# Gathers of a graph kernel's node table, counted on 68 semaphores of their own in turn, with TensorE's wait set by hand

## The chip, the cores and the metric

One Trainium2 chip, of which the kernel uses one core. The metric is the device time of one execution in microseconds (us), as the median of several runs. About 0.2% is what a measurement of this kernel can tell from no change.

The engines are named as in the profile: PE (TensorE) multiplies matrices, PEld is its loading of the stationary operand, DVE (VectorE) and ACT (ScalarE) work elementwise, POOL (GpSimd) here issues gathers, and SP (SyncE) issues plain transfers. Each engine runs its own instructions in order and is tied to the others by semaphores: counters which one side raises and the other waits for.

## The reference

A pre-norm layer of a relational graph network. There are 12500 nodes of 256 features, 212500 edges sorted by their target, and 8 types of edges, each with a 256x256 weight.

```python
hx = jnp.einsum('ni,rio->rno', x, weight)
msg = hx[edge_type, src]
agg = jax.ops.segment_sum(msg, dst, num_segments=num_nodes)
node_repr = agg * jnp.asarray(ALPHA, x.dtype) ** 0.5
node_repr = node_repr + h_bias
loop_message = x @ loop_weight
node_repr = node_repr + loop_message * jnp.asarray(1.0 - ALPHA, x.dtype) ** 0.5
...
h = jnp.maximum(_layernorm(x, axis=-1), 0.0)
x = x + _L0_gnn_ref(edge_index, h, edge_type_8, weight, h_bias, loop_weight)
```

## The kernel before

The kernel turns the order round: it first sums the rows of h over each target's incoming edges, apart for each type, and then multiplies these sums by the weights.

**Tiles.** The edges are cut into 1581 tiles of up to 128 edges; two tiles (PAIR) make a unit that belongs to one stretch of neighbouring targets. For a tile three things are needed. Its 128 source rows of 256 numbers (128 KB) come by a *gather*: one indirect DMA that POOL issues (`gather`, L901, with the DMA at L915), from x for the first 100 tiles, while the table h is still being made, and from h later. A one-hot matrix (`onehots`, L957), made by DVE for four tiles at once, says for each edge which target and type it counts for. Then PE (`edge_sums`, L985) multiplies the two: for each half c of the features one matmul at L1005, so two in the code for a tile. The profile shows four matmuls and four weight loads, since each of these in float32 runs as two. A unit's two tiles sum in one PSUM bank; after the unit DVE adds the bank into the accumulator ring `acc` (`add_sums`, L1021, the addition at L1031).

**Groups.** When a group of 128 targets has all its sums, PE multiplies them by the eight weights and by the self-loop weight (`group_work`, L1172, matmuls at L1187), and DVE adds the result to x and it is stored.

**The order of work** is written out by hand, in one loop over tiles (L1363). At tile t it issues the gathers up to `goal(t)` (L922): 64 tiles ahead until tile 170, then fewer, down to 24 from tile 370 on, and in the last 120 tiles a fifth of what is left, not under 8. A gather of an even tile also waits for the last finished unit (L918-920, "no faster than the sums"). The message buffers hold 66 tiles in pairs.

**Row tiles.** Every 28th tile from tile 167 on (167, 195, ..., 50 in all) is not gathered by POOL. Its 128 rows are fetched by 128 transfers of 1 KB each, half from SP and half from ACT (`load_sources`, `fetch`). They count on four semaphores `rows0` to `rows3`, for which PE waits in an instruction of its own at L1002. So POOL issues 1581 - 50 = 1531 gathers, 1431 of them from h.

**Semaphores of the gathers.** The kernel names none for them. The scheduler under it counts the DMAs of POOL on eight semaphores in turn, and sets a gather's waits itself: for the DMA that counted on the same semaphore before, eight gathers earlier, and for PE where a buffer or the pace asks for it. An instruction holds one wait; a second one becomes an instruction of its own in front of it. The first matmul of a gathered tile waits on the gather's semaphore for its full count (16 for each DMA).

**Runs.** `in_run` (L358) ties the matmuls of a unit together: only the last counts on PE's semaphore, and whoever waits for the unit waits for that count.

Of the kernel before, what the change touches and what calls it, by code (L numbers as in the profile page):

```python
# [66 lines left out]
HOLD = 8  # L67
FAR = 36
COUNTERS = 4


QUAD = 4
# [172 lines left out]
def kernel(  # L245
# [15 lines left out]
    KC = D // P  # L261
# [48 lines left out]
    def place_of(t):  # L310
        u, i = divmod(t, PAIR)
        half = 0 if PAIR * u + 1 == NT else PAIR - 1 - i
        b, row = row_of(u)
        return b, half, row


    with ExitStack() as main:
# [29 lines left out]
        msg, oh, offsets, kind = {}, {}, {}, {}  # L347
        firsts, stops, loops, marked, typed, gidx, col = {}, {}, {}, {}, {}, {}, {}
        added, zeroed = {}, {}
        single, fetches = {}, {SP: [], ACT: []}  # L350
        counters = [tc.alloc_semaphore(f"rows{i}") for i in range(COUNTERS)]
        fetched, summed = {}, {}
        state = {"h32": None}


# [2 lines left out]
        def in_run(kind, i, last):  # L358

            name, count = runs.get(kind, (None, 0))  # L360
            key = f"{kind}{count}"
            if last:
                if name is not None:
                    tc.declare_fence(i.ins, group=key)
                runs[kind] = (None, count + 1)
            else:
                tc.no_tile_sem_insts.add(i.ins.name)
                tc.add_to_no_dep_group(key, i.ins)
                runs[kind] = (key, count)
            return i  # L370
# [508 lines left out]
        def room(t):  # L879

            both = msgs.tile([P, PAIR, D], F32, name="msg")
            for i in range(PAIR):
                msg[t + i] = both[:, i, :]

        def single_rows(t):

            return (t % SINGLE == SINGLE - 1 and t + 2 * NEAR < NT
                    and state["h32"] is not None and t // QUAD * QUAD >= state["h32"] + LATE + AHEAD)

        def begin_fetch(t):  # L890

            if t not in msg:
                room(t - t % PAIR)
            fetched[t] = len(fetched)
            for k, r in enumerate(range(0, P, SOURCES)):
                engine = SP if k in BY_SP else ACT
                fetches[engine].append((
                    done["tile"] + HOLD,
                    lambda r=r, engine=engine: load_sources(t, r, engine)))

        def gather(t):  # L901
            if t % PAIR == 0 and t not in msg:
                room(t)
            if t % QUAD:
                kind[t] = kind[t - 1]
            else:
                kind[t] = "h" if state["h32"] is not None and t >= state["h32"] + LATE else "x"
            table = {"h": h32, "x": x}[kind[t]]
            b, i, u = place_of(t)
            if single_rows(t) and t not in fetched and t - done["tile"] >= FAR:  # L910
                begin_fetch(t)
            if t in fetched:
                return
            at = i * P + u
            i = nc.gpsimd.indirect_dma_start(  # L915
                out=msg[t], out_offset=None, in_=table[:, :],
                in_offset=bass.IndirectOffsetOnAxis(ap=gidx[b][:, at : at + 1], axis=0))
            if "unit" in latest:  # L918
                tc.add_manual_dep(
                    i.ins, latest["unit"], SYNC_DEP, reason="no faster than the sums")  # L920
# [7 lines left out]
        def load_sources(t, r0, engine):  # L928
# [9 lines left out]
            def fetch_row(i, v):  # L938
                j = queue.dma_start(
                    msg[t][r0 + i : r0 + i + 1, :].bitcast(U8), h32_bytes[:, bass.ds(v, D * 4)])  # L940
                j.then_inc(counters[k % COUNTERS], 16)
                tc.no_tile_sem_insts.add(j.ins.name)
                tc.add_to_no_dep_group(f"rows{t}", j.ins)
                if i == 0 and k >= COUNTERS:
                    tc.add_manual_dep(
                        j.ins, summed[k - COUNTERS], SYNC_DEP, reason="counter is at rest")

# [37 lines left out]
        def edge_sums(t):  # L985
            m, o = msg.pop(t), oh.pop(t)
            if t % PAIR == 0:
                bank = banks[t // PAIR % BANKS]
                sums["ps"] = bank[:, : KC * R * WIN].rearrange("p (c k) -> p c k", c=KC)
            ps = sums["ps"]  # L990
            i = t % PAIR
            b, half, _ = place_of(t)
            first, width = (R * n for n in (REACH[half] if b < NB - 1 else (0, WIN)))
            end = t == NT - 1 or i == PAIR - 1
            free = added.get(t // PAIR - BANKS)
            if i == 0 and free is not None and latest["pe"] is not None:
                tc.add_manual_dep(latest["pe"], free.name, SYNC_DEP, reason="bank is free")
            if i == 0 and latest["pe"] is not None:
                tc.add_manual_dep(latest["pe"], made[t], SYNC_DEP, reason="one-hots are made")
            if t in fetched:  # L1000
                k = fetched[t]
                j = nc.tensor.wait_ge(counters[k % COUNTERS], 16 * P * (k // COUNTERS + 1))  # L1002
                tc.declare_fence(j.ins, group=f"rows{t}")
            for c in range(KC):
                j = nc.tensor.matmul(  # L1005
                    ps[:, c, first : first + width], m[:, c * P : (c + 1) * P], o[:, :width],
                    start=(i == 0 and c == 0), stop=(end and c == KC - 1), skip_group_check=True)
                in_run("sums", j, end and c == KC - 1)
            latest["pe"] = j.ins
            if end:  # L1010
                latest["unit"] = j.ins.name
            if t in fetched:
                summed[fetched[t]] = j.ins.name
            return ps

        sums = {}
# [216 lines left out]
        with tc.manual_schedule():  # L1233
# [20 lines left out]
            for t in range(min(STARTED, NT)):  # L1254
                gather(t)
            gathered = min(STARTED, NT)

            for bound, lines in ((low, plan.low), (high, plan.high)):
                whole = small.tile([P, NB], I32, name="whole")
                f = small.tile([P, NB], F32, name="bound_f")  # L1260
# [102 lines left out]
            for t in range(NT):  # L1363
# [3 lines left out]
                while gathered < min(NT, goal(t)):  # L1367
                    gather(gathered)
                    gathered += 1
# [31 lines left out]
                if t % (PAIR * REGS) == 0 and t // PAIR + REGS < NU:  # L1401
                    load_offsets(t // PAIR + REGS)
                ps = edge_sums(t)
                while late and late[0][0] <= t:
                    late.pop(0)[1]()
                    credit -= 0.83
                advance(t)
                while writes and credit > 0:
                    _, cost, f = writes.pop(0)
# [14 lines left out]
                while queue and (budget > 0 and t >= queue[0][0] or t >= queue[0][1]):  # L1424
                    _, _, c, f = queue.pop(0)
# [67 lines left out]
```

## Time and profile before

| | |
|---|---|
| median of 3 runs | 1981.88 us (1979.95 to 1982.96) |
| profiled execution | 1982.09 us, its span 1980.4 us, mean granted clock of TensorE 0.949 |
| DMA of the gathers (queue 0) | 200.77 MB, 34.5% of 16 engines' span |
| DMA issued by SP and ACT (queues 1 and 10) | 76.03 MB, 12.8% |

The page gives for each engine its busy time and share of the span. Its groups of instructions have the form: line, engine, operation, out<-in, how many; then busy time in us, mean ns of one; then the idle time of the engine just before them and the releaser that ended most of it. "issue" as a releaser means that the profile shows nothing that the engine waited for. On POOL the length of a gather is the time in which its descriptors are made, not that of the transfer. Views over a stretch of time give the same for that stretch alone.

### The profile page before, as it was taken

The page shows a single profiled execution, that of the slowest core. Times are in us where ns is not written, and L with a number is a line of the kernel's source. Part 1 is how long each engine was busy: PE and PEld are TensorE (multiplying, and loading weights), DVE is VectorE, ACT ScalarE, POOL GpSimd, SP SyncE. Part 2 cuts the span into 40 slices and gives each one's busy share as a digit, 9 for nine tenths or more (in the row PEclk, how much of TensorE's full clock was granted, in tenths as well). Part 3 has the DMA queues.
Part 4 walks back from the last instruction along what each step waited for, and adds up shares of the span by engine and source line. Part 5 has one row for each costly group of instructions (what it writes and reads, how often), then busy time and mean ns, then how long its engine had stood idle before and what let it go on. Part 6 is the DMA issues. An engine that isn't in the chain of part 4 may idle for free. (4 is left out here: it accounts for less than half of the span.)

```text
span 1980.4 us, 41340 instructions
## 1 busy us (share of the span) xinstructions
PE 1711.7 (86%) x10161; PEld 1473.8 (74%) x10161; DVE 1309.2 (66%) x3272; ACT 159.2 (8%) x334; POOL 1457.9 (74%) x1557
## 2 busy tenths in 40 slices
PE   2348999998899888889998898888989989899998
PEld 1247898997777777778777777777777767687897
DVE  6769767886665677656678565578666567665653
ACT  6777200000000000000000000000000000000000
POOL 7677776677777777777777777777777777777774
PEclk8559999999999999999999999999999999999999
DMA  7993444443444444444434444444444344444432
GB/s 252 358 301 103 126 126 134 140 140 107 138 128 122 149 132 120 141 130 121 149 111 141 132 119 143 141 119 141 129 122 142 109 144 130 120 140 125 127 115 78
DMA packets 158363, 279.45 MB, mean 141 GB/s; under 512 B 35376, under 2 KB 109126, under 8 KB 158118
## 3 DMA queue, kind: packets, MB, share of 16 engines
q0 software_dynamic: 73488, 200.77, 34.5%
q1 hardware_dynamic: 76584, 72.73, 11.9%
q10 hardware_dynamic: 8046, 3.30, 0.9%
q8 instruction: 80, 1.31, 0.3%
q14 instruction: 165, 1.35, 0.2%
HBM read 251.06 MB, written 25.60 MB: 140 GB/s over the span
## 5 line engine op out<-in xcount | busy, mean ns | idle before, releaser
L915 POOL DMA_INDIRECT msg<-h,gidx x1431 | 1361.2, 951 | 458.6 <-issue 335.6
L1005 PEld LDWEIGHTS ps<-oh,msg 128*128 128x128 f32 x6324 | 942.1, 198 | 408.1 <-DMA msg<-h,gidx 258.7
L1005 PE MATMUL ps<-oh,msg 128*128 128x136 f32 (+2 forms) x6324 | 1022.8, 291 | 226.3 <-DMA msg<-h,gidx 139.0
L1187 PE MATMUL po<-w,acc 128*128 128x256 f32 x3136 | 891.0, 389 | 15.4 <-DVE acc L1031 15.3
L1031 DVE TENSOR_TENSOR acc<-acc,ps 128x352 f32 x791 | 408.8, 517 | 413.0 <-PE ps L1005 402.1
L1187 PEld LDWEIGHTS po<-w,acc 128*128 128x128 f32 x3136 | 519.0, 193 | 52.1 <-DVE acc L1031 18.6
L1069 DVE SCALAR_TENSOR_TENSOR acc<-types,pt 128x256 f32<-128x256 bf16 (+1 forms) x688 | 247.3, 411 | 67.6 <-PE pt L1051 61.9
L967 DVE TENSOR_TENSOR oh<-fixed,cols 128x544 f32<-128x544 f32 (+1 forms) x396 | 285.8, 722 | 0.0
L915 POOL DMA_INDIRECT msg<-in_x_dram,gidx x100 | 94.8, 948 | 41.4 <-issue 30.1
L1187 PE MATMUL po<-wl,self_t 128*128 128x256 f32 x392 | 115.5, 420 | 3.5 <-DVE acc L1031 1.8
L1187 PEld LDWEIGHTS po<-wl,self_t 128*128 128x128 f32 x392 | 73.8, 210 | 12.6 <-DVE acc L1031 3.1
L853 ACT ACTIVATE msg<-msg,shift,rstd 128x256 f32<-128x256 f32 x100 | 50.8, 586 | 4.4 <-DVE stats L817 3.6
L853 ACT ACTIVATE xt<-xt,shift,rstd 128x256 f32<-128x256 f32 x98 | 50.0, 587 | 7.0 <-DVE shift L850 6.1
L809 DVE BATCH_NORM_STATS2 stats<-xt 128x6 f32<-128x256 f32 x98 | 34.3, 412 | 23.5 <-DMA xt<-in_x_dram 22.7
L1200 DVE TENSOR_TENSOR xr<-xr,po 128x256 f32<-128x256 f32 x98 | 40.4, 412 | 13.4 <-PE po L1187 12.2
L1123 DVE CAST types<-pt 128x512 bf16<-128x512 f32 x22 | 15.2, 691 | 49.6 <-PE pt L1119 49.6
L1056 DVE COPY self_t<-pt 128x256 f32<-128x256 f32 x98 | 40.7, 415 | 8.5 <-PE pt L1051 5.4
L1051 PE MATMUL pt<-ident,hr 128*128 128x128 f32 x196 | 38.9, 281 | 7.2 <-DMA hr<-h 5.3
L442 DVE TENSOR_SCALAR moves<-fixed 128x271 int32<-128x271 int32 (+1 forms) x90 | 40.6, 452 | 4.4 <-DVE acc L1031 3.0
L1201 DVE TENSOR_TENSOR xr<-xr,po 128x256 f32<-128x256 f32 x98 | 41.2, 421 | 3.4
L444 DVE COPY_PREDICATED fixed<-moves,fixed 128x311 int32<-128x311 int32 (+14 forms) x90 | 38.0, 422 | 3.1
L1051 PEld LDWEIGHTS pt<-ident,hr 128*128 128x128 f32 x196 | 25.6, 153 | 10.6 <-DMA hr<-h 5.6
(162 smaller groups left out, 349.1 us busy)
## 6 DMA issues: line engine op xcount, KB each, us to landing
msg<-h ACTq DMA_DIRECT2D x3200, 1.0 KB
msg<-h SPq DMA_DIRECT2D x3200, 1.0 KB
msg<-h,gidx POOLq DMA_INDIRECT x1431
xt<-in_x_dram SPq DMA_DIRECT2D x24, 512.0 KB
h<-xt SPq DMA_DIRECT2D x24, 512.0 KB
xr<-in_x_dram SPq DMA_DIRECT2D x24, 512.0 KB
hr<-h SPq DMA_DIRECT2D x24, 512.0 KB
out_dram<-xr SPq DMA_DIRECT2D x24, 512.0 KB
```

The costliest lines, as they stand in the source:

```text
L442: nc.vector.tensor_single_scalar(m, packed[:, :n], 1 << (bit + k), op=ALU.bitwise_and)
L853: nc.scalar.activation(row, row, AF.Relu, bias=shift[:n, j : j + 1], scale=rstd[:n, j : j + 1])
L915: i = nc.gpsimd.indirect_dma_start(out=msg[t], out_offset=None, in_=table[:, :], in_offset=bass.IndirectOffsetOnAxis(ap=gidx[b][:, at : at ...
L967: j = nc.vector.tensor_tensor(o[:, k : k + v, :i, :width], iota_f[:, :width].unsqueeze(1).unsqueeze(1).to_broadcast([P, v, i, width]), of. ...
L1005: j = nc.tensor.matmul(ps[:, c, first : first + width], m[:, c * P : (c + 1) * P], o[:, :width], start=(i == 0 and c == 0), stop=(end and ...
L1031: i = nc.vector.tensor_tensor(a, a, ps, op=ALU.add)
L1051: in_run("turns", nc.tensor.transpose(pst[:, c, :n], rows_[:n, c * P : (c + 1) * P], ident[:n, :n]), c == KC - 1)
L1056: nc.vector.tensor_copy(got["self", g][:, :, :n], pst[:, :, :n])
L1069: i = nc.vector.scalar_tensor_tensor(acc[:, :, r, s0 : s0 + n], of, float(r + 1), pst[:, :, :n], op0=ALU.is_equal, op1=ALU.mult)
L1187: i = nc.tensor.matmul(got["out", g][:n], lhs, rhs, start=(r == R and c == 0), stop=(r == R - 1 and c == KC - 1))
L1200: nc.vector.tensor_add(rows_[:n, k, :], rows_[:n, k, :], outs[g % 2][:n, 1, :])
L1201: nc.vector.tensor_add(rows_[:n, k, :], rows_[:n, k, :], got["out", g][:n])
```

## The change

Every gather from h counts its landing on one of 68 semaphores allocated for this, in turn, and no longer on a semaphore of the scheduler; the scheduler is told to set none. The first matmul of its tile (c == 0) waits by hand until that semaphore has reached 16 for each gather that used it so far. To the scheduler this matmul stands for the gather's landing: whoever would have to wait for the gather waits for the matmul. It is taken out of the run "sums"; the tile's second matmul stays in it. Gathers from x and the row tiles are unchanged.

```diff
+LANDINGS = 68
...
+        landings = [tc.alloc_semaphore(f"landed{i}") for i in range(LANDINGS)]
+        landed = {}
...
             i = nc.gpsimd.indirect_dma_start(
                 out=msg[t], out_offset=None, in_=table[:, :],
                 in_offset=bass.IndirectOffsetOnAxis(ap=gidx[b][:, at : at + 1], axis=0))
+            if kind[t] == "h":
+                n = landed[t] = len(landed)
+                i.then_inc(landings[n % LANDINGS], 16)
+                tc.no_tile_sem_insts.add(i.ins.name)
+                tc.add_to_no_dep_group(f"landed{t}", i.ins)
             if "unit" in latest:
                 tc.add_manual_dep(
                     i.ins, latest["unit"], SYNC_DEP, reason="no faster than the sums")
...
                 j = nc.tensor.matmul(
                     ps[:, c, first : first + width], m[:, c * P : (c + 1) * P], o[:, :width],
                     start=(i == 0 and c == 0), stop=(end and c == KC - 1), skip_group_check=True)
-                in_run("sums", j, end and c == KC - 1)
+                if t in landed and c == 0:
+                    n = landed[t]
+                    j.wait_op(landings[n % LANDINGS], 16 * (n // LANDINGS + 1), "sem-ge")
+                    tc.declare_no_dep(
+                        j.ins, group=f"landed{t}", reason="waits for the landing by count")
+                    tc.declare_fence(j.ins, group=f"landed{t}")
+                else:
+                    in_run("sums", j, end and c == KC - 1)
```

## The prediction

> **What bounds the kernel now.** I read the page's engine lines and costliest groups first, then one engine in time.
>
> ```profile
> span 1980.4 us, 41340 instructions
> ...
> PE 1711.7 (86%) x10161; PEld 1473.8 (74%) x10161; DVE 1309.2 (66%) x3272; ACT 159.2 (8%) x334; POOL 1457.9 (74%) x1557
> ...
> L915 POOL DMA_INDIRECT msg<-h,gidx x1431 | 1361.2, 951 | 458.6 <-issue 335.6
> L1005 PEld LDWEIGHTS ps<-oh,msg 128*128 128x128 f32 x6324 | 942.1, 198 | 408.1 <-DMA msg<-h,gidx 258.7
> L1005 PE MATMUL ps<-oh,msg 128*128 128x136 f32 (+2 forms) x6324 | 1022.8, 291 | 226.3 <-DMA msg<-h,gidx 139.0
> ...
> L915 POOL DMA_INDIRECT msg<-in_x_dram,gidx x100 | 94.8, 948 | 41.4 <-issue 30.1
> ```
>
> POOL looks like the less loaded engine (74% against PE's 86%), but PE's largest wait at L1005 is for gathers, and POOL's largest "idle" has no releaser. The timeline of POOL alone explains that. The second gather, which has nothing to wait for, and the last one (start, length, and in brackets the idle time before it):
>
> ```profile
> 6.31 0.95 POOL L915 DMA_INDIRECT msg<-in_x_dram,gidx  x1 [0.30 <-issue]
> ...
> 1957.67 0.95 POOL L915 DMA_INDIRECT msg<-h,gidx  x1 [0.30 <-PE ps L1005]
> ```
>
> A free gather costs 0.95 us and a fixed 0.30 us before it: 1.25 us. The waits from 580 us on (total, times, longest) give the gap with one more digit:
>
> ```profile
> POOL msg L915 <- issue: 261.7, 857, 0.4
> ```
>
> That is 0.305 us. So much before a gather is part of its price, whatever releaser the view names. All 1531 gathers at that price are 1915 us of 1980.4: POOL is nearly full. The same engine by stage, as windows of L915's instructions (columns: length, busy and count, clock, DMA share, GB/s) and as the group row of two stretches (280 to 580, 580 to 1960):
>
> ```profile
> 280.00:380.00 100.00, 66.85 (x71) 1.00 0.47 134
> ...
> 580.00:780.00 200.00, 151.63 (x159) 0.97 0.45 132
> ```
> ```profile
> L915 POOL DMA_INDIRECT msg<-h,gidx x225 | 213.5, 949 | 87.2 <-issue 49.3 <-DMA msg<-h,gidx 21.4 <-PE ps L1005 15.0
> ```
> ```profile
> L915 POOL DMA_INDIRECT msg<-h,gidx x1096 | 1043.3, 952 | 335.5 <-issue 261.7 <-PE ps L1005 33.0 <-DMA msg<-h,gidx 32.6
> ```
>
> From 580 on POOL never pauses: 335.5 - 1096 x 0.305 = 1.2 us over the fixed gaps in 1380 us. From 280 to 580 it does: 87.2 - 225 x 0.305 = **18.6 us**. Nothing behind 580 can make up for a pause of POOL, as it runs at its own pace to the last gather, 22 us before the end.
>
> Does PE follow POOL there? The waits of PE and of its weight loads from 580 to 1960:
>
> ```profile
> PE ps L1005 <- DMA msg<-h,gidx: 128.7, 200, 3.4
> ```
> ```profile
> PEld ps L1005 <- DMA msg<-h,gidx: 236.9, 337, 3.8
> ```
>
> PE stands still 129 to 237 us for gathers in that stretch: it has that much room to go faster when they come sooner.
>
> **What the 18.6 us wait for.** In the program of before every gather from the ninth on waits until the gather eight before it, on the same semaphore, has landed in full; each odd tile's gather has only this wait, an even tile's also the one for the last finished unit of sums (L918-920). POOL's waits from 280 to 580, then one stretch of its timeline:
>
> ```profile
> POOL msg L915 <- issue: 49.3, 148, 2.0
> POOL msg L915 <- DMA msg<-h,gidx: 21.4, 38, 1.9
> POOL msg L915 <- PE ps L1005: 15.0, 34, 1.4
> ```
> ```profile
> 276.99 0.95 POOL L915 DMA_INDIRECT msg<-h,gidx  x1 [0.30 <-PE ps L1005]
> ...
> 288.06 0.94 POOL L915 DMA_INDIRECT msg<-h,gidx  x1 [0.97 <-DMA msg<-h,gidx]
> ...
> 293.47 0.94 POOL L915 DMA_INDIRECT msg<-h,gidx  x1 [1.95 <-issue]
> ```
>
> Less 0.305 each, the labels hold 9.8 us (DMA), 4.6 (PE) and 4.2 (issue). The gather at 288.06 waited for the one at 276.99, so that landed about 10 us after it was issued: eight gathers are 10 us of POOL's work, and a slower landing stops POOL. The PE label I don't believe. PE and POOL up to 285 us, and up to 580:
>
> ```profile
> L1005 PE MATMUL ps<-oh,msg 128*128 128x136 f32 (+1 forms) x674 | 122.1, 322 | 81.9 <-DVE acc L1031 49.2 <-ACT msg L853 32.8
> L915 POOL DMA_INDIRECT msg<-h,gidx x115 | 109.2, 949 | 37.8 <-issue 25.9 <-PE ps L1005 5.4 <-ACT msg L853 1.5
> ```
> ```profile
> L915 POOL DMA_INDIRECT msg<-h,gidx x335 | 317.9, 949 | 123.1 <-issue 73.9 <-DMA msg<-h,gidx 22.3 <-PE ps L1005 19.7
> L1005 PE MATMUL ps<-oh,msg 128*128 128x136 f32 (+1 forms) x1761 | 288.2, 297 | 92.8 <-DVE acc L1031 49.2 <-ACT msg L853 32.8 <-DMA msg<-h,gidx 10.3
> ```
>
> With four matmuls per tile PE is at tile 168 at 285 us; POOL has issued 115 + 100 gathers and passed two row tiles (167, 195): tile 217. By the schedule's lead of 64 the gather of tile 217 belongs to loop step 153: the sums it waits for, of tiles up to 151, were done 16 tiles earlier. At 580 PE is at 440, POOL at 335 + 100 + 11 = 446, allowed 24 ahead. So PE holds back no gather here; its label stands where the landing's last record was missed.
>
> **The change, part by part.**
> - A gather from h counts on its own semaphore and no longer on the eight: the wait for the gather eight before goes. That is the 18.6 us, and up to 1.2 us behind 580 that I leave out. Before 280 the pauses belong to other waits (page groups above: gathers from x, which are unchanged, and the early sums). The extra wait instructions that POOL's sequencer ran for even tiles go too, and are worth nothing: the free gathers above have the same 0.30 us gap.
> - TensorE's wait for the landing stays at the tile's first matmul, where it stood (the L1005 waits above); only the semaphore is another. Cost 0, as long as it is one wait on one instruction.
> - That first matmul leaves the run "sums" and may now count on PE's own semaphore: up to 1431 counts more. The row of an odd tile (its last matmul counts for its unit) and of an even tile (no count), each with the matmul behind it:
>
> ```profile
> 1012.22 0.59 PE L1005 MATMUL ps<-oh,msg 128*128 128x104 f32 x4
> ...
> 1012.64 0.62 PE L1187 MATMUL po<-w,acc 128*128 128x256 f32 x2
> ...
> 1013.10 0.63 PE L1005 MATMUL ps<-oh,msg 128*128 128x136 f32 x4
> ...
> 1013.56 0.59 PE L1187 MATMUL po<-w,acc 128*128 128x256 f32 x2
> ```
>
>   The next work starts 0.42 us after the counting tile began and 0.46 after the other: a count costs nothing to see. The far bound is a full drain: a matmul lasts 0.291 us (page) and four take 0.63, so they start (0.63 - 0.29)/3 = 0.11 apart; waiting for the first one's end adds 0.18 us a tile. I take 0, by the nearer row.
> - 68 semaphores: if each had to be reset by one instruction of the kind POOL waits with, 17 ns in the row below, 1.2 us; taken as 0.
>
> ```profile
> L915 POOLq EVENT_SEMAPHORE  x803: 17/17/5023, 31.6 to 1950.8; - x161
> ```
>
> - DVE, SP and ACT, which overwrite an index tile or a message slot, now wait for the matmul that saw the landing; it ran long before in the same order of tiles. 0.
> - What comes next: gathers are issued 18.6 us, 15 gathers, sooner by 580 us. If PE stayed where it was, POOL would be 6 + 15 = 21 tiles ahead; the limit is 24, so the unit's wait still doesn't bind. Then PE eats the lead up and waits for POOL again, at 1.25 us a gather.
>
> Sum, against the profiled execution's own 1982.09 us (1.7 over its span; 0.2 over the median of 1981.88): 1982.1 - 18.6 = **1963.5 us**.
>
> **The rivals.**
> 1. *Only what is labelled goes.* The PE and issue parts (4.6 + 4.2) have causes of their own that stay; the gap of 1.95 at 293.47 could be one such. 1982.1 - 9.8 = 1972.3. Against it stand the tile counts.
> 2. *Landings set the pace anyway.* Without the brake more gathers queue in front of the same late DMA engine, and PE gets its data no sooner. For: landings of 10 us while the 16 engines are on average only 0.47 busy (windows), so one of them must be late. Against: the same 0.45 behind 580, where 1.25 us a gather is kept up with no pause, so the jam passes; what POOL gains in it is kept. If it does not pass: 1982.
> 3. *The pauses are not waits for landings*, or gathers keep some such wait: POOL stops for something of its own (its instructions, say), and the 49.3 us labelled issue are the clue. Then nothing is removed: 1982. Against: the gather at 288.06 has its releaser, and nothing in the diff leaves a wait. The Trainium skill ("DMA: Bandwidth & Descriptors", Anatomy of one DMA) gives a DMA from GpSimd as about 2.0 us plus its bytes over 436 GB/s, an estimate of 2.3 us for 128 KB, by which a wait over eight gathers would never bind; the row at 288.06 differs from it, and decides.
> 4. *Slower: PE pays at each tile.* The first matmul now carries a wait set by hand and perhaps a count; if the second matmul had to wait for its end, 1431 x 0.18 = 258 us of PE. PE has 139.0 us of idle for gathers (page; 258.7 by its weight loads), so it decides from 139.0/1431 = 97 ns a tile on; at 0.18 us the excess is 258 - 139 = 119: 2101 us. Against: counting and other tiles follow each other alike. The Trainium skill ("TensorE: Matmul & The Clock Gate", The cost: per-tile semaphore tail) says that counts of matmuls in a row serialize at 26.3 ns each; an estimate of 1431 x 26.3 ns = 38 us, 2001 if nothing hid it, though PE's idle would; no row here isolates it.
>
> **How the numbers follow.** Forecast 0.66, rival 1 0.14, rival 2 0.05, rival 3 0.03, rival 4 0.12. The time is the forecast's. Its own range is 1959 (19.8 us, with 3 for the runs' spread of 1979.95 to 1982.96) to 1968. Taking in rival 1 and part gains the range goes to 1978; 0.2 is left out. About 0.2% (4 us) is what a measurement can tell here. Faster: 0.66 + 0.14 = 0.80; same 0.08; slower 0.12.
>
> **What the changed profile would show.** Right: L915's idle from 280 to 580 near 0.305 a gather, no DMA among POOL's releasers of gathers from h beyond that, the 1431 gathers over by about 1940 us, and PE's wait for gathers still there behind 800 us. The wait instructions of POOL's sequencer fall from 803 to few. Wrong: pauses of POOL with the PE label in their place (the lead of 24 binds), gathers longer than 0.95 us, or the four matmuls of a tile spread beyond 0.63 us.

## The result, and the profile after

| | before | after |
|---|---|---|
| median of 6 runs each | 1982.95 us (1979.95 to 1985.77) | 1966.41 us (1962.19 to 1969.06) |
| ratio | | 0.9912, 95% interval 0.9902 to 0.9923 |
| profiled execution | 1982.09 us, span 1980.4 | 1962.19 us, span 1960.5 |

The change makes the kernel 16.5 us faster between the medians, and 19.9 us between the two profiled executions; that of after is the fastest of its six. The page of after, for the lines shown of before:

```profile
span 1960.5 us, 40526 instructions
...
PE 1693.2 (86%) x10161; PEld 1457.9 (74%) x10161; DVE 1308.3 (67%) x3272; ACT 159.2 (8%) x334; POOL 1456.0 (74%) x1557
...
L918 POOL DMA_INDIRECT msg<-h,gidx x1431 | 1359.3, 950 | 438.1 <-issue 370.6
L1013 PEld LDWEIGHTS ps<-oh,msg 128*128 128x128 f32 x6324 | 931.5, 196 | 406.5 <-DMA msg<-h,gidx 251.5
L1013 PE MATMUL ps<-oh,msg 128*128 128x136 f32 (+2 forms) x6324 | 1009.2, 289 | 226.0 <-DMA msg<-h,gidx 131.8
...
L918 POOL DMA_INDIRECT msg<-in_x_dram,gidx x100 | 94.7, 947 | 42.7 <-issue 29.1
```

POOL makes the same 1531 gathers at the same 0.95 us; what shrank is the idle time before those from h, 458.6 to 438.1 us. The shares of busy time tell nothing of it: PE stands at 86% and POOL at 74%, as before. PE's own work was 18.5 us shorter as well, at a mean granted clock of 0.957 against 0.949; its waits below show that this did not set the time. By stage (280 to 580 us, then 580 to 1960), the group rows of POOL's gathers:

```profile
L918 POOL DMA_INDIRECT msg<-h,gidx x239 | 226.9, 949 | 72.9 <-issue 62.9 <-PE ps L1013 7.3 <-PE po L1202 1.2
```
```profile
L918 POOL DMA_INDIRECT msg<-h,gidx x1082 | 1027.6, 950 | 330.1 <-issue 282.1 <-PE ps L1013 40.3 <-PE po L1202 2.7
```

Less the fixed 0.305 us a gather, 72.9 - 239 x 0.305 = 0.0 us of pauses are left between 280 and 580 (before: 18.6), and 0.1 behind (before: 1.2). In the same 300 us POOL issues 239 gathers from h where it issued 225. The waits in that stretch (total, times, longest) show that every label, PE's too, has shrunk to the fixed gap:

```profile
POOL msg L918 <- issue: 62.9, 206, 0.3
POOL msg L918 <- PE ps L1013: 7.3, 24, 0.3
```

The whole difference can be added up from POOL's rows: 18.6 from 280 to 580; 1.1 behind; 1.9 because the gathers from h were busy 1359.3 us and not 1361.2; 0.7 from the gathers from h before 280 (pauses of 2.4 us there, now 1.7, from the groups up to 580 less those from 280); and -1.3 in the gathers from x (41.4 to 42.7). That is 21.0 us. The last gather, which started at 1957.67 us, now starts at

```profile
1936.56 0.94 POOL L918 DMA_INDIRECT msg<-h,gidx  x1 [0.30 <-PE ps L1013]
```

21.1 us sooner. What follows the last gather took 22.7 us and now takes 23.9, so 19.9 us remain.

PE from 580 us on, its matmuls and its weight loads:

```profile
PE ps L1013 <- DMA msg<-h,gidx: 127.4, 204, 2.7
```
```profile
PEld ps L1013 <- DMA msg<-h,gidx: 242.0, 343, 3.1
```

These were 128.7 and 236.9. PE waits for gathers as long as before; it is still POOL's pace that it follows, only the pace started earlier.

### The profile page after: what moved, and what is told of

It reads as the page before. It is cut to its first block, busy times and chain, and to the rows that moved or that the text cites. A ratio compares the mean times of both kernels' runs of the same rounds, so it can differ in the third digit from the quotient of the medians.

```text
span 1960.5 us, 40526 instructions
## 1 busy us (share of the span) xinstructions
PE 1693.2 (86%) x10161; PEld 1457.9 (74%) x10161; DVE 1308.3 (67%) x3272; ACT 159.2 (8%) x334; POOL 1456.0 (74%) x1557
## 5 line engine op out<-in xcount | busy, mean ns | idle before, releaser
L918 POOL DMA_INDIRECT msg<-h,gidx x1431 | 1359.3, 950 | 438.1 <-issue 370.6
L1013 PEld LDWEIGHTS ps<-oh,msg 128*128 128x128 f32 x6324 | 931.5, 196 | 406.5 <-DMA msg<-h,gidx 251.5
L1013 PE MATMUL ps<-oh,msg 128*128 128x136 f32 (+2 forms) x6324 | 1009.2, 289 | 226.0 <-DMA msg<-h,gidx 131.8
L918 POOL DMA_INDIRECT msg<-in_x_dram,gidx x100 | 94.7, 947 | 42.7 <-issue 29.1
L1202 PE MATMUL po<-wl,self_t 128*128 128x256 f32 x392 | 110.7, 406 | 3.4 <-DVE acc L1046 1.8
L1215 DVE TENSOR_TENSOR xr<-xr,po 128x256 f32<-128x256 f32 x98 | 40.4, 412 | 12.5 <-PE po L1202 11.5
```

The source lines that it names most:

```text
L918: i = nc.gpsimd.indirect_dma_start(out=msg[t], out_offset=None, in_=table[:, :], in_offset=bass.IndirectOffsetOnAxis(ap=gidx[b][:, at : at ...
L1013: j = nc.tensor.matmul(ps[:, c, first : first + width], m[:, c * P : (c + 1) * P], o[:, :width], start=(i == 0 and c == 0), stop=(end and ...
L1202: i = nc.tensor.matmul(got["out", g][:n], lhs, rhs, start=(r == R and c == 0), stop=(r == R - 1 and c == KC - 1))
L1215: nc.vector.tensor_add(rows_[:n, k, :], rows_[:n, k, :], outs[g % 2][:n, 1, :])
```

## The experiments

Twelve runs were made, of nine kernels, in three sets. Within a set the kernel before ran on the same chip, and ratios are to it. The first set ran on a chip on which the kernel before took 1981.03 us. The chips of the second and third set were slower: there the kernel before itself took 2427.88 and 2396.80 us. Their times are compared only within their set.

### First set: which part of the change gains the time

**The brake alone, put back.** To the changed kernel a wait is added in front of each gather from h, on the new semaphores:

```diff
+            back = len(landed) - BACK
+            if kind[t] == "h" and back >= 0:
+                nc.gpsimd.wait_ge(landings[back % LANDINGS], 16 * (back // LANDINGS + 1))
             i = nc.gpsimd.indirect_dma_start(
```

With BACK = 8 this is the wait of the program of before, and all else is the changed kernel: SP's and ACT's wait instructions, which also became fewer by the change (230 to 178 and 179 to 127 in the compiled program), stay at the lower number.

> The changed kernel with the brake alone put back: before each gather from h, GpSimd waits until the h gather eight before it has landed, now by the new semaphores; SyncE's and ScalarE's programs stay those of the changed kernel. Theory A (the gain is this wait, 18.6 us between 280 and 580 us): 1982 to 1985 us, ratio to before 0.998 to 1.001, and the idle before gathers from h from 280 to 580 us is again 15 to 22 us over 0.305 us each. Rival B (the gain comes from the waits that left the queues of SyncE and ScalarE, or from fewer instructions of TensorE's tile): about 1966 us, ratio 0.991. Rival C (GpSimd's own 700 wait instructions cost the time, whatever they wait for): also 1982, told apart by the same wait with distance 12.

Measured: 1982.49 us, ratio 1.0012 (1.0001 to 1.0022). POOL's group row from 280 to 580 us and its waits there:

```profile
L922 POOL DMA_INDIRECT msg<-h,gidx x227 | 214.8, 946 | 86.5 <-issue 44.3 <-DMA msg<-h,gidx 24.4 <-PE ps L1017 16.2
```
```profile
POOL msg L922 <- issue: 44.3, 139, 0.8
POOL msg L922 <- DMA msg<-h,gidx: 24.4, 49, 1.6
POOL msg L922 <- PE ps L1017: 16.2, 35, 1.7
```

86.5 - 227 x 0.305 = 17.3 us of pauses are back, and with them the whole gain is gone. Rival B falls. The labels are back in all three kinds, though the only thing that came back is a wait for a landing: a pause labelled "PE" or "issue" (35 x 0.305 = 10.7 of PE's 16.2 us are floor, the rest pauses of up to 1.7 us) was one for a landing too.

**The same wait, longer: BACK = 10 and 12.**

> As the run with distance eight, but each gather waits for the one ten before it. Theory A: in the changed kernel landings came 8 to 11.6 us behind the gather and at most 11 gathers were issued before one landed; ten gathers are 12.5 us of GpSimd's work, so it pauses little, 0 to 3 us: 1966 to 1970 us, ratio 0.991 to 0.994. Rival C: 1982, ratio 1.000.

> As the run with distance eight, but each gather waits for the one twelve before it (15 us of GpSimd's work), with just as many wait instructions. Theory A: never binds, 1964 to 1968 us, ratio 0.991, idle before gathers from 280 to 580 us within 1 us of 0.305 each. Rival C (the instructions cost the time): 1982, ratio 1.000.

Measured: 1965.44 us, ratio 0.9921 (0.9903 to 0.9939), with ten; 1962.93 us, ratio 0.9911 (0.9892 to 0.9929), with twelve. From 280 to 580 us, with ten and with twelve:

```profile
L922 POOL DMA_INDIRECT msg<-h,gidx x240 | 228.3, 951 | 73.2 <-issue 47.3 <-DMA msg<-h,gidx 15.5 <-PE ps L1017 8.8
```
```profile
L922 POOL DMA_INDIRECT msg<-h,gidx x240 | 227.8, 949 | 73.2 <-issue 46.1 <-DMA msg<-h,gidx 14.4 <-PE ps L1017 10.1
...
POOL msg L922 <- DMA msg<-h,gidx: 14.4, 47, 0.3
```

73.2 - 240 x 0.305 = 0.0 us in both. The label "DMA" is there 47 times, at 0.3 us each: here it names the gap that every gather has, and not a pause. And the wait instructions of POOL's sequencer, which are in both kernels (sequencer row of the added line; count, shortest, median and longest in ns):

```profile
L921 POOLq EVENT_SEMAPHORE  x689: 17/17/17, 221.6 to 1927.7; - x173
```

So 689 wait instructions cost nothing that shows when what they wait for has come. Rival C falls; what matters is the distance, and ten gathers (12.5 us of POOL's work) are far enough where eight (10 us) are not.

**TensorE's side alone,** in the kernel before:

```diff
-                in_run("sums", j, end and c == KC - 1)
+                if t in fetched or kind[t] != "h" or c:
+                    in_run("sums", j, end and c == KC - 1)
```

> The kernel before with the change's TensorE side alone: the first matmul of a tile gathered from h no longer belongs to the run, so the scheduler may make it count (205 more matmuls of this program count than before); gathers still wait for the one eight before. Theory A: 1981 to 1985 us, ratio 0.999 to 1.001, TensorE's busy time and mean matmul as before. Rival D (counts cost TensorE time that its waiting hides): the time is the same, but the mean matmul of the edge sums lengthens by 3 ns or more (205 x 0.06 us over 6324). Rival E (a count costs and shows): 2001 us or more.

Measured: 1980.13 us, ratio 0.9996 (0.9986 to 1.0005). POOL's row from 280 to 580 us, and PE's from its page:

```profile
L915 POOL DMA_INDIRECT msg<-h,gidx x225 | 213.5, 949 | 87.2 <-issue 49.1 <-DMA msg<-h,gidx 19.3 <-PE ps L1005 14.5
```
```profile
L1005 PE MATMUL ps<-oh,msg 128*128 128x136 f32 (+2 forms) x6324 | 1020.9, 290 | 229.1 <-DMA msg<-h,gidx 136.6
```

The pauses stay (18.6 us) and the mean matmul is 290 ns, against 291 before: neither cost nor gain. The 0.06 us a count in rival D's sum stands in no run, and that sum gives 1.9 ns and not 3, which is about what the mean differs by between kernels (289 to 291). The trace decides it more closely: behind a first matmul that counts, the tile's next matmul starts 112 ns later with 104 columns and 116 ns with 136, as behind one that doesn't count (medians from 600 to 1800 us; 58 and 52 tiles that count, 437 and 442 that don't). Rivals D and E fall.

### Second and third set: the single rows

These sets were to answer what makes the landings late from 280 to 580 us, and whether still fewer gathers on POOL would help. Only SINGLE is changed, which says that every so-many-th tile is fetched row by row by SP and ACT: 28 in both kernels, 10000 for none, 26, 24 and 20 for more.

```diff
-SINGLE = 28
+SINGLE = 10000
```

> The kernel before without row tiles: GpSimd gathers all 1581 tiles, SyncE and ScalarE fetch no single rows (6400 transfers of 1 KB less). Question: do these transfers make the late landings from 280 to 580 us, on which the wait for the gather eight before catches? 50 more gathers at 1.25 us are 62.5 us. Theory F (they do): pauses gone, 1982 + 62.5 - 18.6 = 2026 us, and the kernel after without row tiles takes the same within 3 us. Rival G (the landings are late for another reason, such as the node blocks' transfers): pauses stay, 2045 us.

> The changed kernel without row tiles. Theory F: 1966 + 62.5 = 2026 to 2029 us, equal to the kernel before without row tiles: nothing is left for the change to remove. Rival G: also 2026 to 2029, but 16 to 19 us under the kernel before without row tiles.

> The changed kernel with every 24th tile fetched row by row and not every 28th: 9 gathers less on GpSimd. If GpSimd's 1.25 us a gather is the pace: 1963 to 1966 less 11.3, so 1952 to 1955 us. Rival (more single rows make landings later still and TensorE waits for the row tiles): 1963 us or more.

> The changed kernel with every 20th tile fetched row by row: 20 gathers less. By GpSimd's pace 25 us less: 1938 to 1941 us. Rival: as for every 24th; above 1950 us shows that the single rows have begun to cost.

The chip ran the kernel before at 2427.88 us, so a third set tried again, and met a chip at 2396.80:

> Again the kernel before without row tiles, since the chip of the first try ran the kernel before itself at 2428 us. By its own kernel before (1981 us on the first chips): Theory F (the single rows make the late landings): 62.5 us for 50 more gathers less the 18.6 us of pauses, ratio 1.022, and no pause over 0.305 us a gather from 280 to 580 us. Rival G (landings late for another reason): ratio 1.032 and pauses of 15 to 20 us.

> Again the changed kernel without row tiles. Theory F: ratio to the kernel before 1.022, the same as the kernel before without row tiles. Rival G: 1.022, where the kernel before without row tiles has 1.032.

> The changed kernel with every 26th tile fetched row by row: 4 gathers less than the changed kernel, 5 us: ratio to the kernel before 0.989 if GpSimd's gathers are the pace and the single rows come in time; above 0.992 if they don't.

> Again the changed kernel with every 24th tile fetched row by row, on another chip than the first try: 9 gathers less, 11.3 us: ratio to the kernel before 0.985 to 0.987 if GpSimd's gathers are the pace; above 0.990 if the single rows come late.

| | second set | third set |
|---|---|---|
| before, no row tiles | 2370.51, ratio 0.9758 (0.9734 to 0.9782) | 2342.49, ratio 0.9776 (0.9753 to 0.9799) |
| after, no row tiles | 2367.92, ratio 0.9739 (0.9713 to 0.9764) | 2341.86, ratio 0.9788 (0.9757 to 0.9818) |
| after, every 26th | | 2460.79, ratio 1.0267 (1.0241 to 1.0293) |
| after, every 24th | 2590.88, ratio 1.067 (1.0643 to 1.0696) | 2558.39, ratio 1.067 (1.0623 to 1.0717) |
| after, every 20th | 2812.58, ratio 1.1582 (1.1548 to 1.1615) | |

The times expected missed, because on these chips something else bounds the kernel. The chain of waits of the changed kernel with every 24th tile fetched by rows, third set (shares of the span by engine, then by line):

```profile
SPq 49%; issue 31%; PE 12%; DVE 3%; DMA 3%; another core or an unknown queue 1%; ACT 1%; DVEq 0%; PEldq 0%; POOL 0%; POOLq 0%; ACTq 0%
SPq L947 40%; SPq L939 7%; PE po L1202 6%; PE ps L1013 6%; DMA xt<-in_x_dram 1%; DMA msg<-h 1%; DVE stats L812 1%; DVE acc L1046 1%; SPq L1152 1%; ACT xt L856 1%; DMA hr<-h 0%; SPq L1221 0%; PE pt L1066 0%; DVE oh L975 0%
```

SP's sequencer, which issues the single rows at L947, is the longest part of the chain. From 960 to 1060 us it issued this many in the changed kernel itself, on its own chip, and in the kernel with every 26th tile by rows, on the third set's:

```profile
L947 SPq DMA_DIRECT2D msg<-h x218: 227/228/762, 959.8 to 1059.9; - x109
```
```profile
L947 SPq DMA_DIRECT2D msg<-h x160: 3/226/736, 959.9 to 1059.0; - x160
```

One instruction takes 0.23 us on both, yet fewer get out, and more are asked for: 26 tiles between row tiles, not 28. So each further row tile costs time there, and none at all is best (ratios of 0.974 to 0.979). POOL pauses too where it has no rows beside it. The kernel of before without row tiles, third set, from 280 to 580 us, and the changed kernel without row tiles in the same set:

```profile
L915 POOL DMA_INDIRECT msg<-h,gidx x203 | 193.4, 953 | 107.0 <-issue 53.3 <-PE ps L1005 27.7 <-remote 24.7
```
```profile
L918 POOL DMA_INDIRECT msg<-h,gidx x204 | 193.5, 948 | 109.3 <-issue 52.3 <-PE ps L1013 30.5 <-remote 22.2
```

45 us of pauses in both (107.0 - 203 x 0.305 and 109.3 - 204 x 0.305: 45.1 and 47.1), with or without the wait of before: these aren't waits for landings. They are waits for PE. In these two kernels, third set, nearly every gather behind a pause of over 1 us from 280 to 1900 us (258 of 260) starts within 0.3 us of an update of PE's semaphore, at the median 0.12 us behind it, and in the changed kernel all but one of those gathers wait for nothing else. In the second set it is 308 of 311. POOL is 18 to 24 tiles ahead of PE when it pauses between 580 and 1800 us, where on the chip of the profiles before and after its lead was 2 to 10: here the schedule's limit of 24 tiles holds it, by the wait for the last finished unit. PE in turn does not wait for gathers: no such wait is among its waits in the changed kernel without row tiles, third set, from 580 to 1960 us. The longest there, of its matmuls and of its weight loads:

```profile
PE ps L1013 <- issue: 126.6, 208, 1.8
```
```profile
PEld ps L1013 <- issue: 169.0, 258, 1.9
```

So without row tiles PE sets the pace on these chips, and the two kernels take the same time (2342.49 and 2341.86; 2370.51 and 2367.92 in the second set). What stops PE, in waits for nothing that the profile shows, stays open. The equal times therefore say nothing on landings: a pace of POOL that nobody waits for can't show what a brake on POOL costs. Nor can the records of the landings, since the traces of the second and third set hold only 20 to 27% of them (97% in the changed kernel on its own chip).

The runs thus leave the question about the single rows open. Theory F can't be told from rival G where POOL, held by PE, takes 1.46 us a gather without row tiles (third set, first to last) and up to 1.84 with every 20th tile by rows. The trace of the changed kernel, on its own chip, goes further: the lateness is that of one part in sixteen. A gather's landing is counted by 16 records. The median time from the end of the gather's instruction to each, in us, over the gathers for which all 16 are in the trace:

```
stretch (us)   gathers   1st   8th   15th   16th
 280 to  420        81   1.5   1.7    1.8    8.5
 420 to  580        86   1.5   1.7    1.8    8.8
 600 to  700        62   1.5   1.6    1.8    5.3
1000 to 1200       120   1.5   1.6    1.8    3.6
```

Fifteen parts of the gather are there 1.8 us after it, in every stage; the sixteenth takes 8.5 to 8.8 us up to 580 us and 3.6 to 5.3 later. The packets of the single rows fit that: from 400 to 412 us those issued by SP and those issued by ACT start one behind the other's end, without overlap, in groups with 0.4 to 1.0 us between them. Each of these gaps is filled by packets of gathers, of which the first starts as the group ends; in six of the eight it is a 4 KB packet that takes 0.6 to 0.8 us, against a median of 0.16 from 280 to 580 us. That looks like one DMA engine shared by the single rows and a sixteenth of each gather, though the trace doesn't name the engine of a packet.

The same trace shows when the sixteenth is late. No single row is issued before 229 us or after 1884 us. For the gathers from h issued from 140 to 227 us the sixteenth record came 1.8 us behind the instruction too (median of 67, at most 4.9), with transfers of the node blocks beside the first of them, and from 1887 to 1928 us 1.8 again (32 gathers, at most 2.6). It was also 1.8 from 1835 to 1884 us, while SP alone issued the last rows. So in this trace the sixteenth is late, in the median, only while SP and ACT both issue rows. This speaks for theory F; a run without rows on that chip, which would test it, wasn't made.

The rows are denser in the stretch where POOL paused. The transfers issued in 300 us of the changed kernel, from 280 on and from 1000 on:

```profile
msg<-h ACTq DMA_DIRECT2D x672, 1.0 KB
msg<-h SPq DMA_DIRECT2D x614, 1.0 KB
msg<-h,gidx POOLq DMA_INDIRECT x239
```
```profile
msg<-h SPq DMA_DIRECT2D x569, 1.0 KB
msg<-h ACTq DMA_DIRECT2D x568, 1.0 KB
msg<-h,gidx POOLq DMA_INDIRECT x239
```

1286 single rows against 1137, beside the same number of gathers: row tiles are begun by PE's tiles, and PE runs through more of them while it eats up its lead. That this makes the difference between 8.5 us and 3.6 is an argument from two counts and not a test.

## Why the prediction was right

- **What bounds the kernel.** POOL's pace, 1.25 us a gather, at 74% busy: right. Where the kernel before takes 1981 to 1983 us, the time follows POOL's pauses in six kernels: 17.3 to 18.6 us of pauses, 1980 to 1983 us; none, 1963 to 1966.
- **The price of the brake, 18.6 us.** Right in place and size: 18.6 became 0.0. The small terms that the sum left out (1.1 behind 580 us, the gathers' own length, the later end) make up the difference to the 19.9 us between the profiles. The forecast of 1963.5 is 1.3 us from the profiled execution and 2.9 under the median; the medians themselves are 16.5 us apart, so the closeness to the profile is in part luck, as that was the fastest of six runs. As a ratio it is 1963.5 / 1982.1 = 0.9906, inside the measured interval.
- **"The PE label I don't believe."** Right. The PE and issue labels fell to the fixed gap with the landing wait gone, and came back with it alone (BACK = 8). With them rival 1 falls. The label is not always wrong: on the slower chips it stands for a true wait for PE. The tile counts tell the two apart.
- **What comes next.** POOL was to run at most 21 tiles ahead, PE then to eat the lead. The changed kernel up to 580 us:

```profile
L918 POOL DMA_INDIRECT msg<-h,gidx x349 | 331.7, 951 | 108.1 <-issue 88.5 <-PE ps L1013 11.6 <-ACT msg L856 1.7
L1013 PE MATMUL ps<-oh,msg 128*128 128x104 f32 (+1 forms) x1813 | 288.4, 292 | 90.4 <-DVE acc L1046 52.3 <-ACT msg L856 32.8 <-DMA msg<-h,gidx 4.3
```

  POOL has passed 349 + 100 + 11 row tiles = 460 tiles, PE 1813 / 4 = 453: a lead of 7. Before, the prediction counted 446 tiles and a lead of 6, with eleven row tiles; but the eleventh is tile 447, so it was 445, and the lead 5. POOL gained 15 tiles by 580 us, PE took up 13 of them at once, and the lead stayed under 10 from 600 to 1800 us.
- **Rival 2, landings set the pace anyway.** It falls by the time, but half of its premise holds: the landings themselves are no sooner. The sixteenth record still comes 8.5 us late, and up to 11 gathers, itself included, are now issued before one lands. The gain came from not waiting for them, as the jam eases by 640 us (median 9.5 us for the gathers from 600 to 620 us, 4.0 from 640 to 660) and PE had the lead to sit it out.
- **Rival 3, no landing waits.** It falls with BACK = 8 and 12. Its page of the Trainium skill ("DMA: Bandwidth & Descriptors", Anatomy of one DMA) gave an estimate of 2.3 us. Fifteen of a gather's sixteen records here come 1.5 to 1.8 us behind the end of its instruction, so about 2.4 to 2.8 behind its start, near that estimate; the sixteenth, at 8.5, doesn't.
- **Rival 4, PE pays at each tile.** It falls by PE's side alone: ratio 0.9996. The premise of "up to 1431 counts more" was too high, too: the scheduler lets only 205 more matmuls of the compiled program count, those that somebody waits for. The Trainium skill's 26.3 ns for a count ("TensorE: Matmul & The Clock Gate", The cost: per-tile semaphore tail), which it gives for matmuls packed side by side in the array, would be an estimate of 5.4 us for these; neither the time nor the spacing of the matmuls (112 and 116 ns with a count and without) shows any of it.
- **Wait instructions worth nothing.** Right. The sequencer's row, x803 before, is now

```profile
L918 POOLq EVENT_SEMAPHORE  x111: 17/17/4997, 31.9 to 1923.8; - x111
```

  and that alone brought nothing, as BACK = 12 shows, which has 689 of them again at 1962.93 us.

Not asked in the prediction was whether the gain holds on another chip. On the two slower chips the changed kernel itself was not run, only its forms with other row tiles; without row tiles the change gains nothing there, since PE and not POOL sets the pace.

## What to carry to other kernels

A queue that is 74% busy can be the pace of everything: multiply its count by its free price (1531 x 1.25 us) before believing the shares, and take a pause for what its stage shows over that floor, not for what the label says. A scheduler's few semaphores in turn are a hidden limit on transfers in flight. When one part in sixteen of a transfer is late, that limit can decide, as here; ask how many more are needed at the peak (here ten are enough), since beyond it further semaphores bought nothing. And ask first who sets the pace: where PE did, on the slower chips, a POOL without the brake was no faster.

## What was not expected of the hardware

- One part in sixteen of a 128 KB gather landed 8.5 us after its instruction (median, 280 to 420 us), the fifteen others by 1.8 us, while the DMA engines' mean busy share was under one half (0.49 from 280 to 380 us).
- Three chips ran the kernel before at 1981.03, 2396.80 and 2427.88 us. On the slower ones PE's mean granted clock was lower (0.876 to 0.889 in the kernel before, against 0.947 to 0.958), single rows left SP at 160 in 100 us where the faster chip had 218, and POOL stopped for about 2 us every ten gathers or so:

```profile
959.23 0.95 POOL L915 DMA_INDIRECT msg<-h,gidx  x1 [2.10 <-remote]
...
973.77 0.95 POOL L915 DMA_INDIRECT msg<-h,gidx  x1 [2.12 <-PE pt L708]
```

  These lines are of the kernel before without row tiles, third set, with nine gathers between them, of which one alone has a gap over 0.31 us (0.50). POOL waits for PE there, as shown above; what stops PE, and what makes SP slower, wasn't found. It changes what a choice is worth: single rows, which take gathers off POOL, cost 2.3 to 2.5% there.
